# A compressed-interaction kernel: the copies that repeat the left-over rows' weights move to a later place in ScalarE's queue

## Chip, cores and metric

The kernel runs on one core of a Trainium2 chip. The metric is the device time of one launch in microseconds (us); lower is better.

## What is computed

For 1024 samples with 39 fields of 64 elements each, three layers combine the fields:

```python
def _cin_layer(Xk, X0, W, b):
    Wr = W.reshape(O, Hk, Fdim)
    return jnp.einsum('bhe,bfe,ohf->boe', Xk, X0, Wr) + b[None, :, None]

Xk = X0                                  # (1024, 39, 64)
for W, b in ((W0, b0), (W1, b1), (W2, b2)):
    Xk = _cin_layer(Xk, X0, W, b)        # (1024, 64, 64)
    outs.append(Xk.sum(axis=-1))
y = jnp.concatenate(outs, axis=-1) @ fc_w.T + fc_b
```

Everything is float32.

## The kernel before

The kernel folds the last two layers and the final row of weights into one table on the 780 products of two fields and the 39 single fields (a single field is stored as a product with a row of ones). So for each block of 32 samples (2048 columns) it multiplies pairs of field rows on VectorE and sums them with weights on TensorE; ScalarE (ACT below) and VectorE (DVE) finish the block.

**Preparation**, to about 17 us. Weights are loaded, combined by matmuls and laid out in `both`, one column per pair of fields. The pairs are dealt out to eight *chunks*. Chunks 0 to 5 (`NPAIR` = 6) have 128 pairs each. What is left over, 32 rows of pairs and 32 of single fields, makes chunks 6 and 7 (`NPAIR`, `NPAIR + 1`), with 32 rows each (`SQUARE` = 32); their work on two blocks at once is split in four row groups, so their weights stand four times in the 128 rows.

**The weights of a chunk** go through three places. `weight_rows(c)` gathers the columns of chunk `c` from `both` into `pairs[:, c]`: on VectorE as sums (line 503, `a != b`), on ACT as copies (line 501, a field with itself or with the ones). For chunks 6 and 7 it also repeats the 32 columns to 64 and then to 128 (line 508, two ACT copies for each chunk). `weight_turn(c)` transposes `pairs[:, c]` on TensorE into a PSUM tile `tr` (line 519) and copies it to `wa[:, c]` with two ACT copies (lines 520 and 521). The matmuls of the chunk (line 535) read `wa[:, c]`. Chunk 6 is all sums (seven on VectorE); chunk 7 is all copies (six on ACT).

**The main loop** runs over `steps`: for an even block `n` the chunks 0 to 6, for the odd block after it the chunks 0 to 5. Step 6 of a pair of blocks is `join`, the matmuls with 32-row weights (lines 555 and 566). A pass `at` issues the matmuls of step `at`, then, for a block that is complete, `finish` and `fields`, and last the VectorE product of step `at + 4` (`AHEAD` = 4; lines 211 and 213) into one of four buffers `p`. A product waits until the matmuls of four steps ago have read its buffer.

In the first passes the weights are still being made. Passes 0, 1 and 2 call `weight_rows` for chunks 4, 5 and 6 ahead of the product (and 7 right behind 6). Passes 2, 3 and 4 call `weight_turn` for chunks 3, 4 and 5, behind the first quarter of their own matmuls; pass 5 calls it for chunks 6 and 7. There is no planner: each engine runs its instructions in the order in which the program gives them, and semaphores join the engines.

**The data.** GpSimd (POOL) issues gathers (line 171) from a transposed copy `xd` of the input into `r` (five tiles for a block, two sets), `u` and `v` (for chunks 6 and 7). `roll(n)` issues the five of block `n`. The loads into `xd` come from POOL and SP queues.

Of the kernel before, what the change touches and what calls it, by code (L numbers as in the profile page):

```python
# [72 lines left out]
NPAIR = len(PAIRS)  # L73
SQUARE = 32
# [70 lines left out]
def cin_kernel(ctx: ExitStack, tc: tile.TileContext, x, w0t, b0, w1, b1, w2, b2, fc_w, fc_b, out):  # L145
    nc = tc.nc
# [13 lines left out]
    def bank(name):  # L160
        return psum.tile([128, MM], F32, name=name, tag="po")

    def load(n, engine=nc.sync):
        first = n % 2 * FT
        engine.dma_start(  # L165
            xd[n // 2 % NTAB][first : first + F].rearrange("f (b e) -> f b e", e=E),
            xv[:, n * BB : (n + 1) * BB, :],
        )
# [6 lines left out]
    def roll(n, tiles=range(NT)):  # L175
        for i in tiles:
            k = n % 2 * NT + i
            gather_rows(rt[n % 2][:, i], xd[n // 2 % NTAB][: FT if k < NT else 2 * FT], k)

    def roll_small(n):  # L180
        table = xd[n // 2 % NTAB].rearrange("f (t c) -> (f t) c", c=SUB)
        for k, dst in enumerate((ut, vt)):
            gather_rows(dst[n // 2 % 2], table, 2 * NT + k)
# [18 lines left out]
    pairs = const.tile([128, NCHUNK, 128], F32, name="pairs")  # L202
    unit = const.tile([128, 128], F32, name="unit")

    def product(n, c, cols=slice(0, BLK), p=None):
        if p is None:
            p = prods.tile([128, BLK], F32, name="p", tag="p")
        if c < NPAIR:
            i, k = PAIRS[c]
            r = rt[n % 2]  # L210
            nc.vector.tensor_tensor(p[:, cols], r[:, i, cols], r[:, k, cols], ALU.mult)  # L211
        else:
            nc.vector.tensor_tensor(p[:, 0:SUB], ut[n // 2 % 2], vt[n // 2 % 2], ALU.mult)  # L213
        return p

    prep = tc.tile_pool(name="prep", bufs=1)
    with prep as prep:
# [44 lines left out]
        for i in range(NT):  # L262
            at = OFFSET[i] - 3 * K + (0 if i < NT - 1 else -F)
# [146 lines left out]
        for s in range(2):  # L410
            for k in range(NW // 2):
                n = min(128, (F - NW * s) * H - k * 128)
# [66 lines left out]
        for k, a in groups:  # L479
            for t in range(2):  # L480
                lo = max(NA * k, a + NQ * t)
                n = a + NQ * t + NQ - lo
# [9 lines left out]
    def weight_rows(c):  # L492
        for at, n, a, b, sa, sb in RUNS[c]:
            out = pairs[:, c, at : at + n]

            def diagonal(p, q, sp, sq):
                at, by = p * FT + q, sp * FT + sq
                return both[:, at : at + by * (n - 1) + 1 : by]

            if b == F or a == b:  # L500
                nc.scalar.copy(out, diagonal(a, b, sa, sb))
            else:
                nc.vector.tensor_tensor(  # L503
                    out, diagonal(a, b, sa, sb), diagonal(b, a, sb, sa), ALU.add
                )
        if c >= NPAIR:
            for n in (SQUARE, 2 * SQUARE):
                nc.scalar.copy(pairs[:, c, n : 2 * n], pairs[:, c, 0:n])  # L508

    turned = []  # L510

    def weight_turn(c):
        place = len(turned) % 4 * 128
        if not place:
            tr = bank("tr")
        else:
            tr = turned[-1]
        turned.append(tr)
        nc.tensor.transpose(tr[:, place : place + 128], pairs[:, c], unit)  # L519
        nc.scalar.copy(wa[:, c, 0 : 2 * H], tr[:, place : place + 2 * H])  # L520
        nc.scalar.copy(wa[:, c, 2 * H :], tr[:, place : place + H])
# [9 lines left out]
    def multiply(n, c, p, quarters=range(BLK // MM)):  # L531
        open_block(n)
        for m in quarters:
            side = m % 2 * H
            nc.tensor.matmul(  # L535
                po[n][m],
                wa[:, c, side : side + 2 * H],
                p[:, bass.ts(m, MM)],
                start=n % 2 == 0 and c == 0,
                stop=n % 2 == 1 and c == NPAIR - 1,  # L540
            )

    def join(n, p):
        open_block(n + 1)

        def tiles(t, side):
            rows = slice(SQUARE * t, SQUARE * t + SQUARE)
            return rows, po[n + t // 2][2 * t % 4 + side]

        for side in range(2):  # L550
            for t in range(4):
                for half in range(2):
                    rows, dst = tiles(t, side)
                    at = (side + half) * H
                    nc.tensor.matmul(  # L555
                        dst[half * H : half * H + H],
                        wa[rows, NPAIR, at : at + H],
                        p[rows, bass.ts(side, MM)],
                        start=t >= 2,
                        stop=t < 2 and half == side,  # L560
                    )
        for t in range(4):
            for side in range(2):
                rows, dst = tiles(t, side)
                half = (1 - side) * H
                nc.tensor.matmul(  # L566
                    dst[half : half + H],
                    wa[rows, NPAIR + 1, H : 2 * H],
                    ut[n // 2 % 2][rows, bass.ts(side, MM)],
                    start=False,  # L570
                    stop=t < 2,
                )

    def fields(n):
        g[n] = []
        for m in range(BLK // SUB):
            gt = work.tile([H + F, SUB], F32, name="g", tag="g")
            nc.scalar.copy(gt[H : H + F], rt[n % 2][0:F, 0, bass.ts(m, SUB)])  # L578
            g[n].append(gt)
# [9 lines left out]
    def finish(n):  # L589
        z = [work.tile([128, MM], F32, name="z", tag="z") for _ in range(BLK // SUB)]  # L590
        then = [finish_bank(n, m, z[m // 2]) for m in range(BLK // MM)]
        for m in range(BLK // MM):
            then[m]()
            if m % 2:
                b_at = n * BB + m // 2 * SB
                nc.vector.tensor_reduce(  # L596
                    sums[:, b_at : b_at + SB],
                    g[n][m // 2].rearrange("p (b e) -> p b e", e=E),
                    AX.X,
                    ALU.add,  # L600
                )
# [12 lines left out]
    def last_weights(pk):  # L614

        nc.tensor.matmul(pk[0:F, 0:1], v2[0:H, 0, 0:F], bias[:, 0:1], start=True, stop=True)
        nc.tensor.matmul(pk[0:1, 1:2], bias[:, 0:1], fc[:, 1:2], start=True, stop=False)
        nc.tensor.matmul(pk[0:1, 1:2], bias[:, 1:2], fc[:, 2:3], start=False, stop=True)
        nc.vector.memset(wfin[0:H], 1.0)
        nc.scalar.copy(wfin[H : H + F], pk[0:F, 0:1])  # L620
        nc.scalar.activation(kfin, pk[0:1, 1:2], AF.Identity, bias=fcb, scale=float(E))
# [10 lines left out]
    for k, (n, c) in enumerate(steps[:3]):  # L632
        p[n, c] = first[k]
        if k != 1:
            weight_rows(c)
        if not k:
            weight_turn(c)
            spin()
        if k < 2:
            for m in range(2):  # L640
                product(n, c, slice(m * MM, (m + 1) * MM), p[n, c])
                if not k and not m:
                    weight_rows(steps[1][1])
        else:
            product(n, c, halves[0], p[n, c])
# [3 lines left out]
    for n, c in steps[:3]:  # L649
        product(n, c, halves[1], p[n, c])  # L650
    n, c = steps[3]
    weight_rows(c)
    p[n, c] = product(n, c)
    for k, (n, c) in enumerate(steps[:3]):
# [5 lines left out]
    for at, (n, c) in enumerate(steps[:-TAIL]):  # L660
        if c == 0 and 2 <= n and n + 4 < NBLK:
            load(n + 4)
        quarters = range(BLK // MM)
        if at < 3:
            quarters = quarters[2:]
        if at < NPAIR and at > 1:
            multiply(n, c, p[n, c], quarters[:1])
            weight_turn(steps[at + 1][1])
            if at == NPAIR - 1:
                weight_turn(NPAIR + 1)  # L670
            quarters = quarters[1:]
        if c == NPAIR:
            join(n, p.pop((n, c)))
        else:
            multiply(n, c, p.pop((n, c)), quarters)
        if not at:
            fields(0)
        if at == NPAIR + 3:
            last_weights(bank("pk"))
        if at - 1 in over:  # L680
            finish(over[at - 1])
            fields(over[at - 1] + 1)
        if at + AHEAD < len(steps):
            n, c = steps[at + AHEAD]
            if at + AHEAD <= NPAIR:
                weight_rows(c)
                if c == NPAIR:
                    weight_rows(c + 1)
            p[n, c] = product(n, c)
            if c == NPAIR - 1 and n + 2 < NBLK:  # L690
                roll(n + 2)
                if n % 2 == 0:
                    roll_small(n + 2)
                if n < 2:
                    load(n + 4, nc.gpsimd)
# [61 lines left out]
```

## Time and profile before

| what | value |
|---|---|
| median of 3 runs | 741.55 us (741.54 to 742.35) |
| profiled execution, its own time | 742.3 us |
| its span | 740.5 us |
| TensorE busy | 731.0 us (99%) |
| VectorE busy | 641.9 us (87%) |
| GpSimd busy | 386.4 us (52%) |
| ACT busy | 167.1 us (23%) |
| mean DMA rate | 266 GB/s |

The profile records one execution. PE is TensorE's matmuls, PEld its weight loads, SP the queue of SyncE. Each matmul of 128x512 float32 appears as two matmul instructions and two weight loads; a step of four quarters has eight. Start times count from the beginning of the span. A row of the timeline may merge several instructions in a row (x2). What stands behind "<-" in brackets is the instruction that ended the engine's idle time, inferred from semaphores.

### The profile page before, as it was taken

Reading aid. Unit: us, or ns where it says so; the run is one execution under the profiler, and the core shown is the slowest. Engines: PE = TensorE matmul, PEld = TensorE weight load, DVE = VectorE, ACT = ScalarE, POOL = GpSimd, SP = SyncE. Lnnn points to the kernel's source line nnn. Section 1 sums busy time; section 2 is a strip of 40 time slices with the busy share of each in tenths; the row PEclk is TensorE's granted clock in tenths of the full one; section 3 lists DMA queues with packets and bytes.
Section 4 is the critical chain, followed back from the end, with each engine's and each line's share of the span. In section 5 each row is a group of like instructions: output and inputs, shape, how many; then the busy total and the mean of one; then the engine's idle time right before and its main releaser. Section 6 shows DMA issues by size and latency. Waiting matters only on the chain.

```text
span 740.5 us, 6425 instructions
## 1 busy us (share of the span) xinstructions
PE 731.0 (99%) x2408; PEld 319.7 (43%) x2408; DVE 641.9 (87%) x521; ACT 167.1 (23%) x244; POOL 386.4 (52%) x256
## 2 busy tenths in 40 slices
PE   9889999999999999999999999999999999999998
PEld 6434444444444444444444444444444444444443
DVE  6968998888988888898888989888899888899885
ACT  3232122221222212122221212222122222212222
POOL 7877453656544475454556545475554557545300
PEclk9999999999999999999999999999999999999999
DMA  9989767967577786768967677795757875666700
GB/s 300 389 274 393 266 253 289 347 242 270 239 274 314 285 291 234 270 247 306 343 245 263 254 269 289 283 327 226 274 243 283 341 274 229 241 251 254 284 1 1
DMA packets 63656, 197.25 MB, mean 266 GB/s; under 512 B 37684, under 2 KB 37733, under 8 KB 43656
## 3 DMA queue, kind: packets, MB, share of 16 engines
q0 software_dynamic: 29040, 186.22, 64.7%
q1 hardware_dynamic: 32894, 8.63, 5.1%
q10 hardware_dynamic: 1690, 1.99, 1.1%
q8 instruction: 19, 0.31, 0.2%
q14 instruction: 13, 0.11, 0.0%
HBM read 196.76 MB, written 10.60 MB: 280 GB/s over the span
## 4 chain that ended last, share of the span: by engine, by line
PE 95%; DVE 3%; issue 1%; ACT 1%; DVEq 0%
PE po L535 88%; PE po L555 4%; PE po L566 2%; DVE p L211 1%; DVE pairs L503 1%; PE pt L454 0%; PE pv L402 0%; PE pv L454 0%; PE pw L413 0%; DVE wide L303 0%; PE idle L279 0%; ACT pairs L508 0%; ACT part L465 0%; PE small L351 0%; DVE g L585 0%
## 5 line engine op out<-in xcount | busy, mean ns | idle before, releaser
L535 PE MATMUL po<-p,wa 128*128 128x512 f32 x1536 | 667.6, 595 | 3.7 <-ACT wa L520 3.7
L211 DVE TENSOR_TENSOR p<-r 128x2048 f32<-128x2048 f32 (+2 forms) x197 | 434.3, 2235 | 78.7 <-PE po L535 78.7
L171 POOL DMA_INDIRECT r<-xd,lists x156 | 308.9, 1980 | 292.9 <-issue 281.5
L535 PEld LDWEIGHTS po<-p,wa 128*128 128x128 f32 x1536 | 290.9, 191 | 375.7 <-issue 352.0
L583 ACT ACTIVATE z<-po,fc0s 64x512 f32<-64x512 f32 x128 | 87.4, 683 | 382.3 <-PE po L566 219.6
L585 DVE SCALAR_TENSOR_TENSOR g<-po,b0s,z 64x512 f32<-64x512 f32 x128 | 95.9, 749 | 9.3 <-ACT z L583 5.3
L578 ACT COPY g<-r 39x1024 f32<-39x1024 f32 x64 | 66.7, 1043 | 152.1 <-DVE sums L596 124.6
L596 DVE TENSOR_REDUCE sums<-g 103x16 f32<-103x1024 f32 x62 | 75.6, 1219 | 2.2
L555 PE MATMUL po<-p,wa 32*64 32x512 f32 x512 | 31.6, 600 | 0.0
L171 POOL DMA_INDIRECT v<-xd,lists x16 | 28.5, 1782 | 4.9 <-issue 4.9
L171 POOL DMA_INDIRECT u<-xd,lists x16 | 28.3, 1772 | 4.9 <-issue 4.9
L213 DVE TENSOR_TENSOR p<-u,v 128x1024 f32<-128x1024 f32 x16 | 19.5, 1217 | 0.0
L555 PEld LDWEIGHTS po<-p,wa 32*64 32x64 f32 x512 | 9.4, 131 | 20.2 <-issue 20.2
L566 PE MATMUL po<-u,wa 32*64 32x512 f32 x256 | 17.0, 587 | 0.0
L566 PEld LDWEIGHTS po<-u,wa 32*64 32x64 f32 x256 | 5.7, 132 | 8.0 <-issue 8.0
L171 POOL DMA_INDIRECT r<-xh,lists x8 | 7.7, 965 | 2.6 <-issue 1.8
L279 PE MATMUL idle<-const-float32-1.0 128*128 128x256 f32 (+1 forms) x16 | 6.5, 555 | 0.8 <-PEq L744 0.8
L503 DVE TENSOR_TENSOR pairs<-both 128x2 f32<-128x2 f32 (+27 forms) x59 | 6.1, 171 | 0.4 <-issue 0.3
L520 ACT COPY wa<-tr 128x128 f32<-128x128 f32 x8 | 2.1, 265 | 15.6 <-PE tr L519 15.6
L165 POOL DMA_DIRECT2D xd<-in_x x5 | 5.3, 1075 | 0.0
L279 PEld LDWEIGHTS idle<-const-float32-1.0 128*128 128x128 f32 x16 | 4.3, 295 | 1.4 <-issue 0.7
L519 PE MATMUL tr<-unit,pairs 128*128 128x128 f32 x8 | 2.7, 339 | 1.5 <-DVE pairs L503 1.1
(101 smaller groups left out, 63.1 us busy)
## 6 DMA issues: line engine op xcount, KB each, us to landing
xd<-in_x SPq DMA_DIRECT2D x26, 312.0 KB
r<-xd,lists POOLq DMA_INDIRECT x156, 8.9
xd<-in_x POOLq DMA_DIRECT2D x5, 312.0 KB, 6.8
w2s<-in_w ACTq DMA_DIRECT2D x1, 624.0 KB
w1s<-in_w ACTq DMA_DIRECT2D x2, 312.0 KB
xh<-in_x ACTq DMA_DIRECT2D x2, 156.0 KB
xd<-xh SPq DMA_DIRECT2D x2, 156.0 KB
u<-xd,lists POOLq DMA_INDIRECT x16, 10.5
```

What stands on the lines that cost most here:

```text
L171: nc.gpsimd.indirect_dma_start(dst, None, table, bass.IndirectOffsetOnAxis(ap=lists[:, k : k + 1], axis=0))
L211: nc.vector.tensor_tensor(p[:, cols], r[:, i, cols], r[:, k, cols], ALU.mult)
L213: nc.vector.tensor_tensor(p[:, 0:SUB], ut[n // 2 % 2], vt[n // 2 % 2], ALU.mult)
L279: nc.tensor.matmul(idle[:, 0:cols], nc.const_aps.tensor(1.0, (128, 128), F32), nc.const_aps.tensor(1.0, (128, cols), F32), start=True, sto ...
L503: nc.vector.tensor_tensor(out, diagonal(a, b, sa, sb), diagonal(b, a, sb, sa), ALU.add)
L535: nc.tensor.matmul(po[n][m], wa[:, c, side : side + 2 * H], p[:, bass.ts(m, MM)], start=n % 2 == 0 and c == 0, stop=n % 2 == 1 and c == NP ...
L555: nc.tensor.matmul(dst[half * H : half * H + H], wa[rows, NPAIR, at : at + H], p[rows, bass.ts(side, MM)], start=t >= 2, stop=t < 2 and ha ...
L566: nc.tensor.matmul(dst[half : half + H], wa[rows, NPAIR + 1, H : 2 * H], ut[n // 2 % 2][rows, bass.ts(side, MM)], start=False, stop=t < 2,)
L578: nc.scalar.copy(gt[H : H + F], rt[n % 2][0:F, 0, bass.ts(m, SUB)])
L583: nc.scalar.activation(z[one], po[n][m][other], AF.Identity, bias=fc0s[other])
L585: return lambda: nc.vector.scalar_tensor_tensor(g[n][m // 2][0:H, at], po[n][m][one], b0s[one], z[one], ALU.add, ALU.mult)
L596: nc.vector.tensor_reduce(sums[:, b_at : b_at + SB], g[n][m // 2].rearrange("p (b e) -> p b e", e=E), AX.X, ALU.add,)
```

## The change

The repeats of line 508 leave `weight_rows` for a function `spread`. Pass 2 calls `weight_rows(6)` only. Pass 4 (`NPAIR - 2`), after the matmuls of step 4 and `weight_turn(5)` have been issued, calls `weight_rows(7)` and then `spread(6)` and `spread(7)`. So the ten ACT copies (six of line 501 for chunk 7, four repeats) stand behind the weight copies of chunks 4 and 5 in ACT's order, and not ahead of both. Pass 5 transposes chunks 6 and 7 as before.

```diff
-        if c >= NPAIR:
-            for n in (SQUARE, 2 * SQUARE):
-                nc.scalar.copy(pairs[:, c, n : 2 * n], pairs[:, c, 0:n])
+
+    def spread(c):
+        for n in (SQUARE, 2 * SQUARE):
+            nc.scalar.copy(pairs[:, c, n : 2 * n], pairs[:, c, 0:n])
...
         if not at:
             fields(0)
+        if at == NPAIR - 2:
+            weight_rows(NPAIR + 1)
+            for k in (NPAIR, NPAIR + 1):
+                spread(k)
         if at == NPAIR + 3:
             last_weights(bank("pk"))
...
             if at + AHEAD <= NPAIR:
                 weight_rows(c)
-                if c == NPAIR:
-                    weight_rows(c + 1)
             p[n, c] = product(n, c)
```

## Prediction

> **What bounds the kernel now.** I read the page first, for the engine that sets the time; then the table of waits, for the places where that engine stands still; then the timeline around the longest of them; then the same stretch by windows, for the granted clock. The head of the page:
>
> ```profile
> span 740.5 us, 6425 instructions
> ...
> PE 731.0 (99%) x2408; PEld 319.7 (43%) x2408; DVE 641.9 (87%) x521; ACT 167.1 (23%) x244; POOL 386.4 (52%) x256
> ```
>
> TensorE has work for 99% of the span, so a gain needs either less matmul work or fewer standstills. The waits (who waited for whom, us in total, times, longest):
>
> ```profile
> DVE p L211 <- PE po L535: 78.7, 78, 4.1
> ...
> ACT pairs L508 <- DVE pairs L503: 5.8, 1, 5.8
> ...
> PEld po L535 <- ACT wa L520: 5.6, 5, 4.5
> ...
> PE po L535 <- ACT wa L520: 3.7, 1, 3.7
> ```
>
> VectorE mostly waits for TensorE. TensorE itself has one long wait: 3.7 us, once, for a weight copy of ACT. Its weight loads show the same wait as 4.5 of 5.6 us. And ACT itself stood 5.8 us, once, ahead of the very copies (L508) that the change moves. The timeline (start, duration, engine, line, what; in brackets the idle time before it) shows that these are one event:
>
> ```profile
> 31.17 0.27 ACT L520 COPY wa<-tr 128x128 f32<-128x128 f32 x1 [4.25 <-PE tr L519]
> ...
> 32.69 0.27 PE L519 MATMUL tr<-unit,pairs 128*128 128x128 f32 x1
> ...
> 36.73 0.61 DVE L503 TENSOR_TENSOR pairs<-both 128x9 f32<-128x9 f32 x7
> ...
> 37.38 0.49 ACT L508 COPY pairs<-pairs 128x32 f32<-128x32 f32 x2 [5.83 <-DVE pairs L503]
> ...
> 37.78 0.68 ACT L501 COPY pairs<-both 128x10 f32<-128x10 f32 x6
> ...
> 38.49 0.49 ACT L508 COPY pairs<-pairs 128x32 f32<-128x32 f32 x2
> ...
> 38.89 0.26 ACT L520 COPY wa<-tr 128x128 f32<-128x128 f32 x1
> ...
> 39.20 2.01 PE L535 MATMUL po<-p,wa 128*128 128x512 f32 x2 [3.66 <-ACT wa L520]
> ```
>
> Chunk 4's transpose (32.69) was in PSUM at 32.96, but its copy to `wa` ran at 38.89, 5.9 us later: it queued behind the repeats of chunk 6's weights. Those waited for VectorE's sums of chunk 6 (L503, done at 37.34), which stand behind the products of chunks 4 and 5. TensorE had used up what it had by 35.5 and waited to 39.20.
>
> By windows (span in us, busy time of PE, PEld, DVE, ACT, POOL, then granted clock, DMA share, GB/s):
>
> ```profile
> 35.50:39.20 3.70, 0.04 (x1) 0.00 (x0) 3.70 (x10) 1.72 (x12) 3.70 (x4) 1.00 0.91 337
> 39.20:42.70 3.50, 3.50 (x5) 1.55 (x6) 1.48 (x1) 0.44 (x3) 3.19 (x5) 0.51 0.71 244
> ```
>
> After the standstill TensorE ran at half clock (0.51) to 42.7, so the wait cost more than its own length.
>
> [...] clock 0.51 from 39.3 to 42.7 after 3.66 us of idleness, and weight loads 0.76 to 1.07 us apart there against 0.43 us at full clock. [...] the copy of `wa` was ready to run at 32.96 and ran last in line. [...]
>
> **The change part by part.** Nothing is added or removed: the same 10 ACT copies and 7 VectorE sums run. VectorE keeps its order, since the sums of chunk 6 stay in pass 2. No DMA is issued by the moved code, and SP's and POOL's queues are not passed by anything. On ACT the 10 copies, 38.98 - 37.38 = 1.6 us in one piece, move from ahead of chunk 4's two weight copies to behind chunk 5's.
>
> *Removed: the wait for chunk 4.* ACT is free at 31.55, so the copies run when the transpose is done, at 33.0, and end by 33.4. TensorE's weight loads show the gain more sharply than its matmuls, whose ends are modelled. They step 0.43 us apart; the last of step 3 starts at 34.52, so the first of step 4 would start at 34.95. It started at 39.20: 4.25 us.
>
> *Removed: the half clock.* From the first load of step 4 to the first of step 5 the trace has 44.12 - 39.20 = 4.92 us. At full clock a step is 8 loads of 0.43 plus a transpose, which adds 0.11 (31.83 to 33.23 is 1.40 where three loads take 1.29): 3.55 us. Difference 1.37 us. [...] Sum: 4.25 + 1.37 = **5.6 us**.
>
> *Added: the copies stand between chunk 5's weight copies and chunk 6's transpose.* Step 4 starting at 34.95 has its transpose load at 35.81 and the transpose done by 36.5, so ACT finishes the two copies of chunk 5 by 37.0. Then come the 10 moved copies, 1.6 us; the sums they need are there from 37.34, and the six copies for chunk 7, now first in line, cover that. They end at 38.6. Step 5 starts with its load at 34.95 + 3.55 = 38.50, and the load of transpose 6 comes two loads later at 39.36. **The slack is 0.75 us**, so this costs nothing; the cover is step 4's last three matmuls. If the slack were gone, transposes 6 and 7 and all later TensorE work would stand behind it: at worst the whole 1.6 us. Below nothing it cannot fall, since TensorE is then continuous. Transpose 7 waits for the copy of chunk 6 (about 0.5 us) now and afterwards.
>
> *What is late next.* Step 5 needs the product of chunk 5, ready at 36.81, for a start at about 38.9: 2.1 us to spare. The first join starts at 48.98 - 5.6 = 43.4; its small product is ready at 38.48. VectorE's next product, block 1 chunk 1, waited 4.06 us for a buffer that step 4 frees; now that buffer is free at about 39.4 and the product follows its predecessor at 40.7. From there VectorE runs ahead with TensorE. The gathers are the remaining supply: those for block 2 are issued from 45.65 after a load that nothing moved touches. In the trace their second tile has landed at 55.83, and the first product that reads it would start at 63.54 - 5.6 = 57.9: 2.1 us to spare before VectorE, and some 9 us before TensorE, four steps behind. The later rows of gathers follow VectorE and have more.
>
> After the join TensorE runs on at 0.43 us a matmul instruction to the end, as the unbroken pieces of the chain show, so the gain at 43 us is kept to the last bank.
>
> **The sum against its own run.** The profiled execution took 742.3 us, its span 740.5, so 1.8 us lie around it. Span after: 734.9; that execution: 736.7. The profiled time is 0.75 us above the median of the three runs (741.55). I take the gain from the median: 741.55 - 5.6 = 735.95, **736.0 us**. The other end, 736.7, is kept for the range, for the extra 0.75 us may be part of the half-clock cost, which other runs may not have.
>
> **The rivals.**
>
> *The clock's part is not regained, or the median run never had it.* [...] Then only the wait goes, 3.7 to 4.25 us: 737.3 to 737.8 us.
>
> *The repeats become the new wait.* Transpose 6 waits for ACT. For it: only 0.75 us of slack, and it rests on modelled transposes. Against it: all its terms but one are spacings of the same trace. It costs up to 1.6 us: 735.95 to 737.6 us.
>
> *The order doesn't matter.* TensorE would wait as long for something else due at 35 to 39 us. Against it: the product of chunk 4 is done at 33.69, that of chunk 5 at 36.81, and the bank sequence is unchanged. It would give 741.5 us.
>
> *Slower: gathers starve block 2.* [...] If each of its seven gathers took the longest issue seen, 5.27 us, plus 0.3 between them, the last would be issued by 45.65 + 6 x 5.57 + 5.27 = 84.3 and land 9.8 us later (as `v` did: 58.12 to 67.89), at 94.1; with its small product of 1.2 us, 95.3. The join of block 2 starts at 93.66, or 88.1 after the change: 7.2 us late, and the half clock comes back with the standstill (1.4); less 5.6 gained, 3.0 slower: about 744.5 us. It decides only once that landing slips past 91 (from 67.9 in the trace). Against it: VectorE's stretch beside these gathers is finishing work for the most part (their issue took 0.94 us there).
>
> **How the numbers follow.** Full gain, 736.0: 0.68. Clock part missing, about 737.5: 0.14. A new wait at transpose 6, about 736.8: 0.13. Order doesn't matter: 0.02. Starved gathers: 0.03. A difference of 0.2%, 1.5 us, is about what a measurement of this kernel can tell. The first three are all faster by more than that: 0.95; the fourth is the same: 0.02; the last slower: 0.03. The range runs from 735.2 (0.75 us below the forecast, the difference between profiled run and median) to 737.8 (the wait alone).
>
> **What would show it.** Right: the 3.7 us row of PE waiting for ACT `wa` and the 5.8 us before L508 gone; clock 1.00 in every window from 23 us to the end; first join load at 43.4; the 4.06 us wait of the product gone; span 734.9. If the moved copies are the new wait, PE or PEld `tr` L519 waits for ACT `pairs` L508 at about 39.4. Half clock at 39 to 43 us despite no wait would break the clock's part. Wait rows from PE or DVE to DMA `r`, `u` or `v` after 55 us would mean the gathers. The forecast is wrong if the first join's load is later than 45.

## The result, and the profile after

The kernel after takes 735.44 us (median of 4 runs, 735.28 to 735.75) where the kernel before takes 741.92 us (4 runs, 741.54 to 742.35): ratio 0.9913, 95% interval 0.9896 to 0.993. That is 6.5 us less; the forecast was 736.0. Lines from 508 on are one higher than before (the repeats are L509, chunk copies to `wa` L521 and L522); 501 and 503 stay.

The head of the page after:

```profile
span 733.6 us, 6425 instructions
...
PE 726.8 (99%) x2408; PEld 317.5 (43%) x2408; DVE 641.1 (87%) x521; ACT 167.1 (23%) x244; POOL 383.9 (52%) x256
```

The same instructions, 6.9 us less span, and TensorE 4.2 us less "busy": 2.0 of them in the stretch that the change touches, where the half clock was (13.36 us before, 11.40 after), and 2.2 ahead of step 3, where nothing was changed. The waits after, from 31 to 50 us:

```profile
PE tr L520 <- ACT wa L522: 0.5, 1, 0.5
ACT pairs L509 <- DVE pairs L503: 0.3, 1, 0.3
...
DVE p L211 <- PE po L536: 0.2, 1, 0.2
```

The 3.7 us of TensorE for `wa` are gone, ACT's 5.8 us ahead of the repeats have become 0.3, and VectorE's 4.1 us for a buffer 0.2. The timeline after:

```profile
31.46 0.27 PE L520 MATMUL tr<-unit,pairs 128*128 128x128 f32 x1
...
31.77 0.27 ACT L521 COPY wa<-tr 128x128 f32<-128x128 f32 x1 [1.45 <-PE tr L520]
...
35.31 0.27 ACT L521 COPY wa<-tr 128x128 f32<-128x128 f32 x1 [3.16 <-PE tr L520]
...
35.58 0.69 ACT L501 COPY pairs<-both 128x10 f32<-128x10 f32 x6
35.94 0.61 DVE L503 TENSOR_TENSOR pairs<-both 128x9 f32<-128x9 f32 x7
...
36.57 0.89 ACT L509 COPY pairs<-pairs 128x32 f32<-128x32 f32 x4 [0.30 <-DVE pairs L503]
...
38.12 0.14 PEld L520 LDWEIGHTS tr<-unit,pairs 128*128 128x128 f32 x1 [0.24 <-issue]
```

Chunk 4's weights are copied 0.3 us after its transpose starts (6.2 us before). The moved copies fill ACT's idle time behind chunk 5's, the six for chunk 7 cover the wait for VectorE's sums but for 0.30 us, and the repeats end at 37.46, ahead of the load of chunk 6's transpose at 38.12, which waits for nothing. The same two windows as before:

```profile
35.50:39.20 3.70, 3.32 (x9) 1.28 (x7) 3.70 (x10) 1.94 (x14) 2.39 (x5) 1.00 1.02 430
39.20:42.70 3.50, 3.41 (x23) 1.44 (x31) 3.35 (x3) 0.42 (x3) 0.68 (x1) 1.00 0.89 289
```

TensorE is busy for 3.32 us where it was for 0.04, and the clock stays at 1.00.

**Where the 6.9 us lie.** TensorE's weight loads have one order in both kernels, so they can be laid side by side. The first loads of steps 3, 4 and 5 and of the join, before:

```profile
31.49 0.19 PEld L535 LDWEIGHTS po<-p,wa 128*128 128x128 f32 x1 [0.32 <-ACT wa L520]
...
39.20 0.43 PEld L535 LDWEIGHTS po<-p,wa 128*128 128x128 f32 x2 [4.49 <-ACT wa L520]
...
44.12 0.19 PEld L535 LDWEIGHTS po<-p,wa 128*128 128x128 f32 x1 [0.24 <-issue]
...
48.98 0.23 PEld L555 LDWEIGHTS po<-p,wa 32*64 32x64 f32 x16 [0.76 <-issue]
```

and after:

```profile
30.26 0.19 PEld L536 LDWEIGHTS po<-p,wa 128*128 128x128 f32 x1 [0.32 <-ACT wa L521]
...
33.72 0.19 PEld L536 LDWEIGHTS po<-p,wa 128*128 128x128 f32 x1 [0.24 <-issue]
...
37.26 0.19 PEld L536 LDWEIGHTS po<-p,wa 128*128 128x128 f32 x1 [0.24 <-ACT pairs L509]
...
42.13 0.23 PEld L556 LDWEIGHTS po<-p,wa 32*64 32x64 f32 x16 [0.76 <-DVE p L211]
```

The first load of step 3 comes 1.23 us earlier after (30.26 for 31.49), that of step 4 5.48 us earlier (33.72 for 39.20), that of step 5 6.86 us earlier (37.26 for 44.12), that of the join 6.85 us earlier (42.13 for 48.98), and so it stays to the end. The stretch from the first load of step 3 to that of the join measures the change by itself: 17.49 us before, 11.87 after, **5.62 us**. The other 1.23 us were there before any instruction of the change.

### The profile page after: what moved, and what is told of

Same layout as the page of the kernel before. It is cut to its first block, busy times and chain, and to the rows that moved or that the text cites. A ratio compares the mean times of both kernels' runs of the same rounds, so it can differ in the third digit from the quotient of the medians.

```text
span 733.6 us, 6425 instructions
## 1 busy us (share of the span) xinstructions
PE 726.8 (99%) x2408; PEld 317.5 (43%) x2408; DVE 641.1 (87%) x521; ACT 167.1 (23%) x244; POOL 383.9 (52%) x256
## 4 chain that ended last, share of the span: by engine, by line
PE 96%; DMA 3%; DVE 0%; issue 0%; ACT 0%; POOL 0%
PE po L536 90%; PE po L556 4%; PE po L567 2%; DMA r<-xh,lists 1%; DMA xh<-in_x 1%; DMA w2s<-in_w 1%; DMA xd<-xh 0%; DVE p L211 0%; POOL r L171 0%; PE tr L520 0%; DVE g L586 0%; DVE sums L608 0%; ACT z L584 0%; ACT wa L521 0%; DVE y L715 0%
## 5 line engine op out<-in xcount | busy, mean ns | idle before, releaser
L171 POOL DMA_INDIRECT r<-xd,lists x156 | 300.2, 1924 | 286.8 <-issue 275.1
L171 POOL DMA_INDIRECT u<-xd,lists x16 | 33.4, 2086 | 4.9 <-issue 4.6
L521 ACT COPY wa<-tr 128x128 f32<-128x128 f32 x8 | 2.1, 266 | 16.9 <-PE tr L520 16.9
## 6 DMA issues: line engine op xcount, KB each, us to landing
u<-xd,lists POOLq DMA_INDIRECT x16, 10.6
```

The source lines that it names most:

```text
L171: nc.gpsimd.indirect_dma_start(dst, None, table, bass.IndirectOffsetOnAxis(ap=lists[:, k : k + 1], axis=0))
```

## The experiments

My theory (A) was that one wait on ACT's queue, with the half clock after it, is what the change removes, and that the 1.23 us are chance. The rivals: that the number of copies ahead of chunk 4's counts, and not the wait among them; that any place behind chunk 4's copy does; that the moved copies have room to spare; that the half clock has another cause; that the kernel after starts faster for a reason of its own.

All experiments' times spread widely: the kernel before itself took 739.6 to 750.8 us there (67 runs of the first four experiments). The profiles show where that comes from: the first load of step 3 falls anywhere from 30.26 to 43.58 us, and from there to the end of the span the kernel after takes 703.38 us in both of its profiles, as do two of the variants below (e4 and e6). So the stretch just defined is what the experiments are read by.

**Both kernels again** (no edit).

> The kernel before, unchanged, profiled a second time. Theory A (the change is worth 5.6 us in the stretch from 24 to 44 us[...]): the wait of 3.7 us and the half clock after it are here again or nearly so; the preparation's weight loads may lie elsewhere by up to 2.5 us at 15 us. Theory B (the kernel after reaches the main loop sooner every time, for a reason of its own): the preparation has the same half-clock stretch at 18.8 to 22.2 us and the same late loads (first load of line 474 at 15.6 us). Ratio 1.000 to the kernel before under both.

> The kernel after, unchanged, profiled a second time. Theory A: no wait of TensorE for ACT over 0.5 us in the main loop, clock full from about 23 us on; the first load of line 474 may be anywhere from 13.1 to 15.6 us[...]; median gain over the kernel before between 5.6 and 6.8 us. Theory B: first load of line 474 at 13.1 us again, and the gain at 6.5 us in every round.

Before again: 745.6 us median, ratio 0.9997 (0.9974 to 1.002) to the kernel before. After again: 744.0 us, ratio 0.9972 (0.9937 to 1.0006). Here the times do not tell the two kernels apart: the gain in the medians is 2.0 us, where I had expected 5.6 to 6.8 for the kernel after. In the profile of before again, step 0 starts at 30.48 us, not at 19.88: between 17 and 26 us ACT, VectorE and TensorE stand still in turn, and the trace names no instruction of the program as the cause (after again: step 0 at 27.08). TensorE then works at half clock to 35.8 us (0.52 from 30 to 36 us) and is the late one, so the wait is short. The timeline of before again:

```profile
46.47 0.49 ACT L508 COPY pairs<-pairs 128x32 f32<-128x32 f32 x2 [2.89 <-DVE pairs L503]
...
47.98 0.26 ACT L520 COPY wa<-tr 128x128 f32<-128x128 f32 x1
...
48.29 1.13 PE L535 MATMUL po<-p,wa 128*128 128x512 f32 x2 [0.72 <-ACT wa L520]
```

The sums end at 46.44, and step 4's first load comes 1.85 us later, exactly as in the first profile (37.35 and 39.20). But TensorE's last load of step 3 is at 46.54 here, where it had come 2.8 us before the sums ended. The stretch takes 12.86 us before again and 11.87 after again: the change is worth 1.0 us in such an execution. My expectation for A, the wait "here again or nearly so", was wrong: it depends on which of VectorE and TensorE is late.

As for the preparation: the first load of line 474 is at 15.6 us before and 15.6 before again, 13.1 after and 13.6 after again. Alone that would speak for the rival. But variants with the order of before fall elsewhere (14.6 us in e5, 13.8 in e9, 13.6 in e11), so that order alone doesn't decide it.

**Half of the move.**

```diff
 # e3: chunk 7's copies in pass 4, chunk 6's repeats in pass 2
             weight_rows(NPAIR + 1)
-            for k in (NPAIR, NPAIR + 1):
-                spread(k)
+            spread(NPAIR + 1)
...
                 weight_rows(c)
+                if c == NPAIR:
+                    spread(c)
 # e4: chunk 6's repeats in pass 4, chunk 7's copies in pass 2
-            weight_rows(NPAIR + 1)
-            for k in (NPAIR, NPAIR + 1):
-                spread(k)
+            spread(NPAIR)
...
                 weight_rows(c)
+                if c == NPAIR:
+                    weight_rows(c + 1)
+                    spread(c + 1)
```

> Of the moved copies only those for chunk 7 (six of line 501, two repeats) go to pass 4; chunk 6's two repeats stay in pass 2. Theory A (ACT is held by the wait for VectorE's sums of chunk 6, and what stands behind that wait is late): TensorE still waits for chunk 4's weight copy, less by the eight copies that no longer stand ahead of it, 38.98 - 37.87 = 1.1 us: a wait of about 2.6 us; the half clock may or may not come. 739.5 to 741 us. Rival (the number of ACT copies ahead of the weight copy is what counts): eight of ten copies gone take away most of it, 737 us or less.

> The other half: only chunk 6's two repeats go to pass 4; chunk 7's six copies and two repeats stay in pass 2, right behind chunk 3's weight copies, where they wait for nothing. Theory A: the eight copies run at 31.5 to 32.7 us while ACT was idle, chunk 4's weight copy is on time, and the time is that of the kernel after within 0.3 us. Rival (the number of copies counts): the larger part of the cost stays, 739 us or more.

Times: only chunk 7 moved 745.3 us, ratio 0.9985 (0.9961 to 1.001); only chunk 6 moved 744.75 us, ratio 0.9977 (0.9952 to 1.0001). Stretches: 11.86 and 11.87 us. Neither stretch is longer than that of the kernel after (11.87), and the time of e3 misses the 739.5 to 741 us that I had expected. In the profile of e3 TensorE was late, so the wait shrank to 0.2 us. What that profile says is the distance: the first load of step 4 (43.09) comes 0.74 us after the sums end (42.35), not 1.85. With only chunk 6 moved, ACT's timeline is

```profile
44.26 0.49 ACT L509 COPY pairs<-pairs 128x32 f32<-128x32 f32 x2
45.09 0.27 ACT L521 COPY wa<-tr 128x128 f32<-128x128 f32 x1 [0.35 <-PE tr L520]
...
48.64 0.27 ACT L521 COPY wa<-tr 128x128 f32<-128x128 f32 x1 [3.17 <-PE tr L520]
...
48.91 0.51 ACT L509 COPY pairs<-pairs 128x32 f32<-128x32 f32 x2
```

Chunk 7's eight copies ran in time that ACT had free, and chunk 4's copy came 0.3 us after its transpose, 2.8 us before the sums ended (47.92). VectorE was the late one here, its sums ending 1.3 us after TensorE's last load of step 3 (46.62), and still step 4's first load came at 47.05, one step of 0.43 us behind that load. So the two repeats that wait for the sums do the harm, and the other eight only lengthen it.

**Work for TensorE in the wait.**

```diff
+        if at == 3:
+            for _ in range(12):
+                nc.tensor.matmul(turned[-1][:, 384:512], unit, unit, start=True, stop=True)
```

> The kernel before with 12 matmuls of 128 columns more on TensorE behind step 3, about 3 us of work that nobody reads, in the place where TensorE waits for chunk 4's weight copy. Theory A (the wait costs its 4.25 us, and 1.37 us more because it sets the clock down): where the wait is as long as in the first profile, the clock stays at full, step 4 takes 3.55 us from its first weight load to that of step 5 (4.92 before), and the stretch from the first load of step 3 to that of the join takes 16.1 us in place of 17.5; where the preparation leaves TensorE late and the wait is short anyway, the filler costs up to its own 3 us. Rival (the half clock has another cause): half clock after 39 us in spite of the filler, stretch 17.5 us or more.

748.6 us, ratio 1.0056 (1.002 to 1.0091); stretch 15.65 us. It told nothing of the clock: the fillers, written into the tile `tr`, waited for ACT's copies out of that tile and then ran on top, 44.30 to 47.2 us. TensorE was late here too, so the wait that they were to fill was short.

**One pass earlier.**

```diff
-        if at == NPAIR - 2:
+        if at == NPAIR - 3:
```

> The ten copies are given to ACT in pass 3, behind chunk 4's weight copies alone and ahead of chunk 5's. Theory A: chunk 4 is on time, but now chunk 5's weight copy waits for VectorE's sums of chunk 6: the first load of step 5 comes 1.85 us after those sums end, as that of step 4 did before. With the sums at the place that they have in the profile after (0.72 us ahead of that load), 1.1 us are lost against the kernel after: stretch from the first load of step 3 to that of the join 13.0 us (11.9 after, 17.5 before). Where TensorE is late against VectorE it loses less. Rival (any place behind chunk 4's copy does): stretch 11.9 us.

745.4 us, ratio 1.0002 (0.998 to 1.0025). In its profile the stretch is 11.87 us, nothing lost: the sums ended at 36.72 and step 5's first load came at 40.81, 4.1 us later, so nothing had to wait. My 1.1 us needed the timing of the first profile and weren't seen; whether pass 3 loses there is open.

**The slack.**

```diff
...
+            for _ in range(12):
+                nc.scalar.copy(spare, unit)
             weight_rows(NPAIR + 1)
```

> The kernel after with 12 more ACT copies of 128x128 that nobody reads, 2.0 to 2.6 us, just ahead of the moved ones in pass 4. Theory A: the slack before the transpose of chunk 6 is 0.66 us in the profile after; the rest, 1.3 to 1.9 us, is lost: that transpose's load waits for ACT's repeats, stretch 13.2 to 13.8 us. Rival (the moved copies have ample room): stretch 11.9 us as after.

747.6 us, ratio 1.0011 (0.9975 to 1.0047); stretch 13.92 us, 2.05 more than after and a little over the 13.2 to 13.8 expected. The waits of that profile:

```profile
PEld tr L520 <- ACT pairs L509: 2.7, 1, 2.7
...
PE tr L520 <- ACT pairs L509: 1.8, 1, 1.8
```

The 12 copies took 3.9 us, not 2.0 to 2.6; the transpose of chunk 6 waited for ACT's repeats and its load came 2.4 us late. This is the rival "the repeats become the new wait", brought about: the room is small, and with it gone the loss lands on TensorE.

**Chunk 7's transpose one quarter later.**

```diff
+            quarters = quarters[1:]
             if at == NPAIR - 1:
+                multiply(n, c, p[n, c], quarters[:1])
                 weight_turn(NPAIR + 1)
-            quarters = quarters[1:]
+                quarters = quarters[1:]
```

> The kernel after with the transpose of chunk 7 one quarter later than that of chunk 6, which it follows at once in the kernel after and waits about 0.74 us of weight-load time for ACT's copy of chunk 6. Theory A: the wait is hidden behind the quarter's two matmul instructions, 0.6 us less, stretch 11.3 us; it would beat both kernels by what one profile shows but a time barely can. Rival (the wait moves to the join, which needs chunk 7's weights): stretch 11.9 us.

743.8 us, ratio 0.994 (0.9902 to 0.9979) to the kernel before; stretch 11.18 us, 0.69 us less than the kernel after (0.6 expected). The weight loads of its timeline:

```profile
46.86 0.14 PEld L520 LDWEIGHTS tr<-unit,pairs 128*128 128x128 f32 x1 [0.24 <-issue]
47.29 0.30 PEld L536 LDWEIGHTS po<-p,wa 128*128 128x128 f32 x2 [0.29 <-issue]
48.03 0.14 PEld L520 LDWEIGHTS tr<-unit,pairs 128*128 128x128 f32 x1 [0.44 <-ACT wa L522]
```

Two loads of the quarter now lie between the transposes. It is the better version by its profile; its time can't be told from that of the kernel after (ratio of that to the kernel before 0.9972, 0.9937 to 1.0006, in its own runs).

**Late sums.** The four last runs lengthen the wait by work on VectorE:

```diff
...
+            if at + AHEAD == NPAIR:
+                for m in range(2):
+                    nc.vector.tensor_tensor(spare, rt[0][:, 0, halves[m]], rt[0][:, 1, halves[m]], ALU.mult)
             if at + AHEAD <= NPAIR:
                 weight_rows(c)
```

in the kernel before (e9), the kernel after (e10), before with 12 fillers on TensorE in a bank of their own (e11), and with only chunk 7 moved (e12).

> The kernel before with two VectorE products of 128x1024 that nobody reads (2.4 us) ahead of the sums of chunk 6 in pass 2, so that the wait is long even where the preparation leaves TensorE late. Theory A: the first load of step 4 comes 1.85 us after those sums end (as in both profiles of the kernel before), 3.7 us later than it would; TensorE then stands still for over 3 us and the clock goes to half, so that step 4 takes 4.9 us in place of 3.55; stretch from the first load of step 3 to that of the join 11.9 + 3.7 + 1.4 = 17.0 us. Rival (half clock does not follow from the wait): step 4 at 3.55 us, stretch 15.6 us.

> The same two VectorE products ahead of the same sums in the kernel after. Theory A: nothing of TensorE waits for the sums before the transpose of chunk 6, and that has room for them: stretch 11.9 us as in the kernel after, full clock, some 5 us less than with the order of before. Where the sums end later than 1.7 us before that transpose's load, what is lacking is lost, up to 1 us. Rival (the sums matter for another reason, by the products behind them): stretch 13 us or more.

> The kernel before with the two VectorE products and, behind step 3, 12 matmuls of 128 columns that nobody reads, about 2.9 us, in a PSUM bank of their own (the earlier filler wrote into the tile of the transposes and so waited for ACT itself). Theory A: TensorE is at work in the wait, the clock stays full, step 4 takes 3.55 us, stretch 15.6 us, 1.4 us less than without the filler. Rival: half clock all the same, 17.0 us; or the filler runs past the wait and costs its own time.

> Only chunk 7's copies moved, with the two VectorE products ahead of the sums. Theory A (the wait for the sums holds ACT, the copies only add their length): the first load of step 4 comes 0.74 us after the sums end, as in the run of only chunk 7 (1.85 with all ten copies ahead): a wait of 2.6 us, 1.1 us less than with the order of before. Rival (the number of copies counts): a wait of 0.8 us or less.

The delay was larger than I had meant. The two products read tiles of `rt[0]` that `roll(2)`, given a pass earlier, overwrites, so they waited for those gathers: 22.1 us in e9, 11.4 in e10. Sizes in the expectations therefore fail, all four; the distances hold. The timeline of e9:

```profile
60.95 0.61 DVE L503 TENSOR_TENSOR pairs<-both 128x9 f32<-128x9 f32 x7
...
61.60 0.49 ACT L508 COPY pairs<-pairs 128x32 f32<-128x32 f32 x2 [27.95 <-DVE pairs L503]
62.00 0.68 ACT L501 COPY pairs<-both 128x10 f32<-128x10 f32 x6
...
62.70 0.49 ACT L508 COPY pairs<-pairs 128x32 f32<-128x32 f32 x2
63.11 0.26 ACT L520 COPY wa<-tr 128x128 f32<-128x128 f32 x1
```

and of e12:

```profile
59.80 0.61 DVE L503 TENSOR_TENSOR pairs<-both 128x9 f32<-128x9 f32 x7
...
60.45 0.49 ACT L509 COPY pairs<-pairs 128x32 f32<-128x32 f32 x2 [24.41 <-DVE pairs L503]
60.85 0.26 ACT L521 COPY wa<-tr 128x128 f32<-128x128 f32 x1
```

From the sums' end to step 4's first load:

| order of ACT's copies | profile | sums end | first load of step 4 | distance |
|---|---|---|---|---|
| all ten ahead of chunk 4's | before | 37.35 | 39.20 | 1.85 |
| | before again | 46.44 | 48.29 | 1.85 |
| | e9 | 61.56 | 63.41 | 1.85 |
| | e11 | 57.83 | 59.69 | 1.86 |
| chunk 6's two ahead | e3 | 42.35 | 43.09 | 0.74 |
| | e12 | 60.41 | 61.16 | 0.75 |
| chunk 7's eight ahead | e4 | 47.92 | 47.05 | -0.87 |
| none ahead | after | 36.54 | 33.72 | -2.82 |
| | e10 | 55.83 | 42.48 | -13.35 |

With chunk 6's repeats ahead, step 4 is tied to the sums; without them it is not, even when the sums come 13 us later. (In after again, e6, e7 and e8, with none ahead, TensorE was late, and the distance of 0.54 us is its own.) In e10 TensorE went on through step 4 and a quarter of step 5 and stopped only at the transpose of chunk 6 (56.41), for 8.9 us; in e9 it stopped ahead of step 4, for 25.8. Medians: e9 764.6 us, ratio 1.025 (1.0178 to 1.0321) to the kernel before; e10 755.2, 1.015 (1.0088 to 1.0213); e11 762.9, 1.0245 (1.018 to 1.031); e12 760.0, 1.0201 (1.0141 to 1.0261). The 9.4 us between e9 and e10 are not the worth of the order alone, because the sums were not held up equally long in the two.

On the clock, e11 by windows (span, then busy PE, PEld, DVE, ACT, POOL, clock, DMA share, GB/s):

```profile
41.60:44.60 3.00, 3.00 (x26) 2.76 (x24) 0.00 (x0) 0.00 (x0) 0.05 (x1) 1.00 0.72 220
44.60:47.20 2.60, 0.27 (x3) 0.08 (x1) 0.00 (x0) 0.00 (x0) 1.99 (x3) 0.99 1.09 241
47.20:59.50 12.30, 0.00 (x0) 0.00 (x0) 4.64 (x11) 1.54 (x11) 5.71 (x6) 0.50 0.99 386
```

The clock is full while the fillers run and half from 47.2 us on, 2.3 us after the last of them (44.87). In the profile before, without them, it halved at 39.30, 3.8 us after TensorE's last matmul (35.54). As this delay differs from run to run, the clock of e11 may have halved at 47.2 without the fillers too: that they held it isn't shown. In the main loop the half clock followed the standstills of 3.66 us (before, clock 0.51), 14.8 (e11, 0.58 from 59.70 to 65.10 us), 25.8 (e9), 8.9 (e10) and 21.1 (e12; in these three weight loads lie 0.85 or 0.86 us apart). It did not follow those of 0.7 us (before again, clock 1.00), 0.8 (e5) and 1.8 (e7; in these two the loads lie 0.43 us apart). That the clock's 1.37 us vanish with the wait left in place wasn't brought about: no filler fitted its wait.

## Why the prediction was right

**The wait, 4.25 us.** Measured by the loads: the lead grows from 1.23 to 5.48 us between the first loads of steps 3 and 4, 4.25.

**The half clock, 1.37 us.** From step 4's to step 5's first load the lead grows by 1.38. That the half clock would go with the wait was my estimate, and it did: 1.00 from 35.50 to 42.70 us. Both terms came from spacings within one trace, and they held to hundredths. One reading beside them was off: the 1.07 us between loads at half clock is the distance of a row that merges two loads (41.00 and 41.22 us); between rows of one they came 0.76 to 0.85 us apart. The sum doesn't use it.

**The slack, 0.75 us.** It was 0.66 (37.46 to 38.12), as the repeats still waited 0.30 us for the sums. e7 shows what stands behind it.

**What is late next: nothing.** The first join was forecast at 43.4 us; take the 1.23 us of the preparation off and that is 42.1, measured 42.13. The gathers for block 2 were not hurt: the last, `v`, landed at 63.93 (67.89 before), although one issue took 5.95 us, longer than any I had priced. That VectorE's products lengthen an issue, which the rival of starved gathers took for granted, isn't shown: beside one, an issue took 2.31 us (62.16 in the profile before), beside another 0.94 (69.71). Of the rivals, the clock came back, order mattered, and no gather starved.

**What the sum left out.** The span fell by 6.9 us and the median time by 6.5, where 5.6 was forecast for both. In the span the missing term is the preparation, which I took as fixed. TensorE's 28 matmuls of lines 413 and 454 took 6.3 us before (9.39 to 15.71) and 3.8 after (9.42 to 13.21); loads of line 474 came 2.5 us earlier, of which 1.23 reached step 3. The low end of the range had 0.75 us for such differences. Whether the same made up the 0.9 us in the median times is not settled by four runs of each; the loads of line 474 in e5, e9 and e11 show that the order of the copies alone doesn't decide when the preparation ends. That the median lies inside the range, 0.24 us above its low end, owes something to luck.

**What I had not seen** is that the wait's length belongs to the execution. The old order loses (sums' end minus last load of step 3) + 1.85 - 0.43 us. In the first profile that is 2.83 + 1.42 = 4.25. (That is what the order costs ahead of step 4; the half clock comes on top where it follows.) Where TensorE is late, VectorE waits for the buffers that TensorE frees (1.0 us for a product in e10, 1.3 in e5), and the sums end 0.11 us before the last load of step 3 (before again 0.10, after again, e3, e6, e7 and e8 0.11 each): 1.3 us at the load, 1.0 over the stretch. So the change is worth 5.6 us where VectorE is late by 2.8 us, as in the first profile, and about 1 us where it isn't late. That the result was taken from executions of the first sort, like the profile that I priced, was luck too: in all twelve later profiles TensorE stood still for 3.8 to 11.6 us between 15 us and its first load of step 0 (1.1 in the profile before, 1.0 after), and of those in which nothing was added on VectorE only e4 has VectorE late, by 1.3 us.

## What to carry to other kernels

In a queue that runs in order, as ACT's did here (chunk 4's copy was ready at 32.96 us and ran at 38.89), look for an instruction that waits for another engine and ask what stands behind it: the cost is not its own length but how far the engine it waits for lies behind. Move the waiting instruction to just ahead of its own reader, behind everything that an earlier step needs, and reckon the room left there. Before calling the gain a constant, ask which engine is late in the stretch, because a delay elsewhere can hide or bare the wait.

## What the runs showed of the hardware

**The preparation ran at two speeds.** In the profile before, the matmuls of line 454 take 0.74 us each (median) and their weight loads 0.33, from 11.2 to 15.7 us; after, 0.45 and 0.19, from 10.6 to 13.2. The first record of the granted clock in the trace, at full, stands at 15.41 us before and at 9.67 after. What decides when this comes isn't shown. As before and after each came within 0.5 us of their own first load of line 474 when run again (15.6 and 15.6, 13.1 and 13.6), that the kernel has no part in it isn't shown either.

**The length of a standstill alone didn't decide whether the clock went to half.** It did so at 39.30 us, 3.8 us after TensorE's last matmul (before), and at 47.2, 2.3 us after it (e11), but in the first steps also at 18.82, 0.8 us after it (before, 0.50 to 22.24), and at 16.50, 1.0 us after it (after, 0.50 to 19.91). It stayed full through a standstill of 1.8 us in e7, as the loads 0.43 us apart behind it show. What else enters isn't shown.

**The start of this program stalled in some executions.** Ahead of step 0 TensorE stood still once for 8.2 us in before again, 6.9 in after again, 5.0 in e3 and 11.6 in e4, and the trace names no instruction that released it. In before again VectorE (4.2 us) and ACT (6.4) stood too, while GpSimd issued seven gathers of 0.93 or 0.94 us each between 17.73 and 26.1. The first load of step 0 came at 30.48 us in before again and at 27.08 in after again, against 19.88 before and 17.33 after. The cause is open.
